# First attention: the products for one slot's maxima and for the next step of softmax put into shared four-bank tiles, five to a slot

## The chip, the cores and the metric

One core of a Trainium2 chip runs the whole program. The metric is the device time of one execution in microseconds (us), the median of several executions. Engines are named as in the profile: PE (TensorE, matrix products; PEld is its weight load), DVE (VectorE), ACT (ScalarE), POOL (GpSimd) and SP (the queue that issues most DMAs). SBUF is the on-chip memory that all of them read and write; PSUM is the memory that PE writes, in eight banks of 512 float32 columns on 128 partitions.

## What is computed

Two layers, each with an attention and a mixture of experts, on x of 8 batches x 512 tokens x 256 features, in float32. The change is in the first layer's attention, a causal softmax attention with 16 heads of 16 features:

```
xn = layernorm(x)
q, k, v = heads(xn @ Wq.T), heads(xn @ Wk.T), heads(xn @ Wv.T)   # 16 heads of 16
scores = where(causal, (q @ k.T) / 4, -inf)                      # 8 x 16 x 512 x 512
attn = softmax(scores, axis=-1)
x = x + (attn @ v) @ Wo.T + ffn(xn)                              # ffn: 8 experts, 2 a token, and a shared one
...                                                              # the second layer
```

The second layer is a gated linear attention, with experts of its own. It is the same in both kernels.

## The kernel before

**Slots.** The first attention is worked in 32 slots (`N = B * NG`): one slot is four heads of one batch. The four heads of a slot sit on four groups of 32 partitions of `q` and `k` (16 features, a row for the maximum, zeros), so that four products of 32 rows run on PE side by side. The loop (L1172) runs n from -1 to 32; in the part for n it takes the maxima of slot n + 1, the softmax weights of slot n, and its average.

**Two passes over the scores.** `maxima(n, j)` (L955) makes the scores of query tile j (128 queries) against its (j + 1) x 128 keys: four products, a head each (L961), then four products of an identity with a mask in bfloat16 that add a large negative number above the diagonal (L965). DVE takes the maximum over the keys (L966). `shift(n)` (L968) turns the four tiles' maxima on PE (L972) and subtracts them from q's spare rows on DVE (L978). `probs(n, i)` (L981) makes the transposed, shifted scores of key tile i against the 512 - 128 i queries from it on (L987), ACT takes exp from PSUM into SBUF (L991), and POOL clears what lies above the diagonal (L993). `average(n)` (L1004) multiplies the four exp tiles with v (L1011). `scaled(n)` (L1023) divides by the row sums on DVE, one slot later.

I write m3 to m0 for the maxima products of query tiles 3 to 0 (512, 384, 256, 128 keys), s0 to s3 for the weight products of key tiles 0 to 3 (512, 384, 256, 128 queries), and `red` and `exp` for the DVE and ACT instructions that read them.

**One PSUM tile.** All these scores go through the pool `l0sc`, which has one buffer (`bufs=1`) of four banks, a head to a bank. Every `maxima` and every `probs` takes it as a new tile, so PE may write the next one only when DVE or ACT has read the last one. In a slot the tile turns over eight times: m3, s0, m2, s1, m1, s2, m0, s3. The other four banks (`l0mm`) hold everything else, a bank each.

**What fills the gaps.** Between these steps the loop puts other work into the program: `fill(each)` takes steps from the list `between` (norms, router, values, output projections, the experts' second products gdn, L692, and the shared expert's, sdn, L1094, transposes xgTp, L600), seven times in a slot. After them come the projections qk (L931) of slot n + 2, the experts' first products gup (L659) or sup (L1071) and the average. `move(...)` lets POOL issue the indirect DMAs of the routing, after the last POOL mask. The order that each engine gets is made from this by a scheduler when the program is built: it moves single products of the filler in between, and it puts a wait before any instruction that writes a tile which another engine still reads. Each engine then runs its list strictly in order.

**ACT's tables.** exp and gelu (L677, L1078) use different tables of ACT. Where one follows the other, an ACT_TABLE_LOAD stands before it.

Of the kernel before, what the change touches and what calls it, by code (L numbers as in the profile page):

```python
# [8 lines left out]
F32 = mybir.dt.float32  # L9
# [3 lines left out]
ALU = mybir.AluOpType  # L13
AX = mybir.AxisListType
PSUM = bass.MemoryType.PSUM

B, S, D = 8, 512, 256
P = 128
NT = S // P
# [6 lines left out]
H0, HD0 = 16, 16  # L26
# [58 lines left out]
def tile_two_layers(  # L85
# [22 lines left out]
    nc = tc.nc  # L108
# [96 lines left out]
    last = {}  # L205
# [6 lines left out]
    @contextmanager  # L212
    def behind(*engines):
        with ExitStack() as stack:
            for e in engines:
                if e in last:
                    stack.enter_context(tc.issue_after(last[e].ins))
            yield
# [636 lines left out]
    with tc.tile_pool(name="l0w", bufs=1) as awp, tc.tile_pool(  # L855
        name="l0", bufs=2
    ) as ap, tc.tile_pool(name="l0e", bufs=2) as wp, tc.tile_pool(
        name="l0sc", bufs=1, space=PSUM
# [9 lines left out]
        mxs, vaugs = [], []  # L868
# [27 lines left out]
        N = B * NG  # L896
# [13 lines left out]
        def values(b, t):  # L910
            ps = ps_mm.tile([P, S], F32, tag="mm", name=f"v{b}_{t}")
            for k in range(KD):
                nc.tensor.matmul(
                    ps[:, :D],
                    xnT[b][:, k, t * P : (t + 1) * P],
                    wv[:, k, :],
                    start=(k == 0),
                    stop=(k == KD - 1),
                )
            nc.scalar.copy(  # L920
                vaugs[b % 2][:, t, : H0 * W].rearrange("p (h c) -> p h c", c=W)[:, :, :HD0],
                ps[:, :D].rearrange("p (h d) -> p h d", h=H0),
            )
# [28 lines left out]
                        raws[which][at + HD0 * h : at + HD0 * (h + 1), :],  # L952
                    )

        def maxima(n, j):  # L955
            w = (j + 1) * P
            q, k = qs[n % 2], ks[n % 2]
            ps = ps_sc.tile([P, 4, S], F32, tag="sc", name=f"m{n}_{j}")
            for h in range(4):
                r = slice(32 * h, 32 * h + 32)  # L960
                nc.tensor.matmul(  # L961
                    ps[:, h, :w], q[r, j * P : w], k[r, :w], start=True, stop=False
                )
            for h in range(4):
                nc.tensor.matmul(ps[:, h, j * P : w], ident_h, mask_lt, start=False, stop=True)  # L965
            last["dve"] = nc.vector.tensor_reduce(mxs[n % 2][:, j, :, HD0], ps[:, :, :w], AX.X, ALU.max)  # L966

        def shift(n):  # L968

# [8 lines left out]
            nc.vector.tensor_sub(q, qs[n % 2], ps)  # L978
            shifted[n] = q

        def probs(n, i):  # L981
            w = S - i * P
            q, k = shifted[n], ks[n % 2]
            ps = ps_sc.tile([P, 4, S], F32, tag="sc", name=f"s{n}_{i}")
            for h in range(4):
                r = slice(32 * h, 32 * h + 32)
                nc.tensor.matmul(  # L987
                    ps[:, h, :w], k[r, i * P : (i + 1) * P], q[r, i * P :], start=True, stop=True
                )
            e = ap.tile([P, 4, w], F32, tag=f"pt{i}", name=f"pt{n}_{i}", bufs=1)  # L990
            nc.scalar.activation(e, ps[:, :, :w], AF.Exp, scale=0.25)  # L991

            last["pool"] = nc.gpsimd.affine_select(  # L993
                out=e[:, :, :P],
                in_=e[:, :, :P],
                pattern=[[0, 4], [1, P]],
                base=0,
                channel_multiplier=-1,
                compare_op=ALU.is_ge,
                fill=0.0,  # L1000
            )
            pts[n, i] = e
# [20 lines left out]
        def scaled(n):  # L1023

            b, g = divmod(n, NG)
            if g == 0:
                oTs[b] = ap.tile([P, KD, S], F32, tag="oT", name=f"oT{b}", bufs=1)
            ou = ous.pop(n)
            den = ap.tile([P, S // 32], F32, tag="den", name=f"den{n}", bufs=1)
            nc.vector.reciprocal(den, ou[:, :, HD0])  # L1030
            nc.vector.tensor_mul(ou, ou, den.unsqueeze(2).to_broadcast([P, S // 32, 32]))
            rd = ap.tile([P, S], F32, tag="rd", name=f"rd{n}", bufs=1)
            nc.vector.transpose(rd, ou.rearrange("p n c -> p (n c)"))
            for h in range(4):
                at = (g % 2 * 4 + h) * HD0
                nc.sync.dma_start(
                    oTs[b][at : at + HD0, g // 2, :], rd[32 * h : 32 * h + HD0, :]
                )
# [80 lines left out]
        def groups_of(n):  # L1119
            if n < FIRST:  # L1120
                return [shared.popleft() for _ in range((2, 0, 0, 1, 2, 2, 2, 2, 1)[n + 1])]
            if n <= LAST:
                have = NG_MAX - len(experts)
                want = -(-NG_MAX * (n + 1 - FIRST) // (LAST + 1 - FIRST))
                return [experts.popleft() for _ in range(want - have)]
            return [shared.popleft() for _ in range(min(1, len(shared)))]
# [14 lines left out]
        def fill(n):  # L1141
            for _ in range(n):
                if between:
                    between.popleft()()

        def move(n):
            for _ in range(n):
                if moves:
                    with behind("pool"):
                        moves.popleft()()  # L1150
# [21 lines left out]
        for n in range(-1, N + 1):  # L1172
            b, g = divmod(n, NG)
            steps = []
            for _ in range(6 if n >= 0 else 2):
                if norms:
                    steps.append(norms.popleft())
            if n == 2:
                steps.append(routing)
            if n >= 1:  # L1180
                steps.append(lambda n=n: scaled(n - 1))
            if g == 1 and b + 1 < B:
                steps += [lambda b=b, t=t: values(b + 1, t) for t in range(NT)]
            for group in downs:
                steps += down_steps(group)
            groups = groups_of(n)
            if n == FIRST:
                loading()
            steps += [lambda i=i: routed.turn(i) for kind, i in groups if kind == "routed"]
            if n >= NG and g == 0:  # L1190
                steps += [lambda b=b, t=t: out(b - 1, t) for t in range(NT)]
            if n == -1:
                steps += [s for group in groups for s in up_steps(group)]
            if n == LAST + 2:
                move(len(moves))
                for i in range(2):
                    ask(i)
            if n > LAST + 1:
                steps += turn1_steps(ps_mm)
                for i in ((0,), (1, 2), (3, 4), (5, 6))[n - LAST - 2]:  # L1200
                    steps.append(lambda i=i: late(lambda: route0.add(i)))
                    if i + 2 < B:
                        steps.append(lambda i=i: ask(i + 2))
                    steps += [lambda s=s: late(s) for s in norm1_steps(i, ap)]
            if n == N:
                steps.append(lambda: route0.add(B - 1))
            between.extend(steps)
            each = -(-len(steps) // 7) if steps else 0
            pace = 2 if n < FIRST else 1

            if n == 10:
                load_second()
            if 0 <= n < N:
                shift(n)
            for s in range(NT):
                if n + 1 < N:
                    maxima(n + 1, NT - 1 - s)
                    move(pace)
                    fill(each)
                if 0 <= n < N:  # L1220
                    probs(n, s)
                    move(1)
                    if s < NT - 1:
                        fill(each)
            fill(len(between))
            if n + 2 < N:
                if n % 2 == 0:
                    for which in range(2):
                        project(n + 2, which)
                spread(n + 2)  # L1230
            elif n + 2 == N:
                with behind("spread"):
                    load_wcat()
            for group in groups:
                if n >= 0:
                    for step in up_steps(group):
                        step()
                kind, i = group
                if kind == "routed" and i in nxt:
                    routed.load(nxt[i])  # L1240
            if FIRST < n <= FIRST + CLEAR:
                clear(1, n - FIRST - 1)
            downs = groups
            if 0 <= n < N:
                average(n)
# [334 lines left out]
    with tc.tile_pool(name="m1w", bufs=4) as wp, tc.tile_pool(  # L1580
        name="m1", bufs=2
    ) as mp, tc.tile_pool(
        name="m1u", bufs=4, space=PSUM
    ) as ps_up, tc.tile_pool(name="m1d", bufs=2, space=PSUM) as ps_dn, tc.tile_pool(
        name="m1p", bufs=2, space=PSUM
# [105 lines left out]
```

## Time and profile before

| | |
|---|---|
| median of 8 executions | 1937.51 us (1934.67 to 1949.11) |
| the profiled execution | 1935.15 us, of which 1933.1 us are the span from the first to the last instruction |
| first attention, first to last slot | about 56 to 1019 us of the span |
| PE busy over the span | 1799.9 us (93%) |
| DVE, ACT, POOL busy | 831.2, 793.5, 401.1 us (43, 41, 21%) |
| granted PE clock, mean | 0.975 |

The profiled execution is 2.4 us below the median. In the profile's answers a group of instructions has its source line, its engine, what it writes and reads, a count, the busy time, the mean time of one in ns, and after the last bar the idle time of its engine just before it with what ended it. PE shows two records for a float32 product, one for a bfloat16 product or a transpose. A window gives the busy time of each engine in a stretch of the span, then the granted PE clock as a share of full speed.

### The profile page before, as it was taken

What the parts mean: (1) busy time and instruction counts of PE and PEld (TensorE: products, weight loads), DVE (VectorE), ACT (ScalarE), POOL (GpSimd) and SP (SyncE); (2) the same over time, 40 slices, a digit from 0 to 9 for tenths busy, and PEclk for the clock granted to TensorE, in tenths of its full rate; (3) what the DMA queues carried; (4) which work ended last, traced back from release to release, by engine and by line L of the source; (5) the groups of instructions that cost most, each with busy time, mean ns of one, the idle gap of its engine ahead of it and who ended that gap; (6) DMA issues with size and microseconds to landing.
All of it is one profiled execution on the core that took longest, in us unless ns stands there. A gap on an engine that the chain in (4) does not pass through costs nothing. (4 is left out here: it accounts for less than half of the span.)

```text
span 1933.1 us, 28227 instructions
## 1 busy us (share of the span) xinstructions
PE 1799.9 (93%) x10680; PEld 1232.0 (64%) x10680; DVE 831.2 (43%) x1886; ACT 793.5 (41%) x1452; POOL 401.1 (21%) x457
## 2 busy tenths in 40 slices
PE   5988999999999999999868899999999999999898
PEld 3434665666666665665434455598888998896455
DVE  5463334434444434444485877521111111115865
ACT  2333353454245445344443465342323233235455
POOL 2015441121122121121123274111111111111000
PEclk9998999999999999999879899999999999999999
DMA  8824221656534433342342141376676777662500
GB/s 244 196 56 134 84 90 46 202 161 185 178 121 134 148 121 134 105 158 73 115 145 68 45 142 59 108 256 231 229 274 216 258 261 250 218 259 82 163 12 23
DMA packets 163687, 289.17 MB, mean 150 GB/s; under 512 B 63952, under 2 KB 134624, under 8 KB 152928
## 3 DMA queue, kind: packets, MB, share of 16 engines
q1 hardware_dynamic: 148432, 248.77, 40.2%
q0 software_dynamic: 13088, 36.07, 5.2%
q10 hardware_dynamic: 2032, 2.54, 0.4%
q8 instruction: 84, 1.38, 0.3%
q14 instruction: 51, 0.42, 0.1%
HBM read 206.78 MB, written 67.94 MB: 142 GB/s over the span
## 5 line engine op out<-in xcount | busy, mean ns | idle before, releaser
L659 PE MATMUL gup<-xgT,ew 128*128 128x256 f32 (+1 forms) x2080 | 386.1, 338 | 4.7 <-DMA ew<-in_dram 2.4
L692 PE MATMUL gdn<-ew,hgT 128*128 128x256 f32 x1640 | 376.4, 383 | 0.0
L659 PEld LDWEIGHTS gup<-xgT,ew 128*128 128x128 f32 x2080 | 331.8, 192 | 47.5 <-issue 7.6
L692 PEld LDWEIGHTS gdn<-ew,hgT 128*128 128x128 f32 x1640 | 307.7, 191 | 50.8 <-issue 11.5
L966 DVE TENSOR_REDUCE mx<-m 128x4 f32<-128x2048 f32 (+3 forms) x128 | 190.3, 1486 | 270.6 <-PE m L965 270.4
L991 ACT ACTIVATE pt<-s 128x2048 f32<-128x2048 f32 (+3 forms) x128 | 158.3, 1237 | 196.4 <-PE s L987 195.8
L719 POOL DMA_INDIRECT zd<-yo,row x144 | 140.3, 974 | 466.8 <-DVE yo L710 403.7
L993 POOL TENSOR_SCALAR_AFFINE_SELECT pt<-pt 128x512 f32<-128x512 f32 x128 | 81.7, 638 | 664.6 <-ACT pt L991 664.6
L670 ACT ACTIVATE hgT<-gup,ew 128x256 f32<-128x256 f32 (+1 forms) x376 | 133.6, 422 | 208.9 <-issue 123.3
L710 DVE SCALAR_TENSOR_TENSOR yo<-ew,way,yo 128x256 f32<-128x256 f32 x72 | 31.7, 482 | 299.6 <-ACT yo L708 299.6
L961 PE MATMUL m<-k,q 32*128 32x512 f32 (+3 forms) x1024 | 124.5, 489 | 23.8 <-ACT pt L991 19.0
L437 POOL DMA_INDIRECT xd<-xr,pos x128 | 128.1, 1000 | 47.0 <-issue 41.9
L987 PE MATMUL s<-qsh,k 32*128 32x512 f32 (+3 forms) x1024 | 112.3, 496 | 25.2 <-DVE mx L966 24.7
L991 ACT ACT_TABLE_LOAD x52 | 66.7, 1283 | 118.7 <-PE s L987 117.8
L961 PEld LDWEIGHTS m<-k,q 32*128 32x128 f32 x1024 | 48.8, 186 | 82.1 <-ACT pt L991 53.8
L1011 PE MATMUL av<-pt,vaug 128*32 128x256 f32 (+3 forms) x1024 | 91.2, 459 | 5.9 <-POOL pt L993 5.7
L987 PEld LDWEIGHTS s<-qsh,k 32*128 32x128 f32 x1024 | 42.9, 191 | 82.7 <-DVE mx L966 63.9
L1020 DVE STREAM_TRANSPOSE ou<-av 128x512 f32<-128x512 f32 x32 | 22.9, 717 | 143.2 <-PE av L1011 143.1
L708 ACT ACTIVATE yo<-gdn,way 128x256 f32<-128x256 f32 x72 | 30.2, 472 | 125.9 <-PE gdn L692 125.7
L1433 PE MATMUL a<-qb,qkTs 128*128 128x512 f32 x128 | 67.3, 608 | 5.7 <-DVE qb L1426 3.7
L1419 PE MATMUL d<-u,cs 128*128 128x512 f32 x128 | 68.7, 619 | 3.9 <-ACT u L1402 3.9
L1402 ACT ACTIVATE u<-cs,lf 128x128 f32<-128x128 f32 x224 | 72.2, 394 | 0.0
(254 smaller groups left out, 2341.3 us busy)
## 6 DMA issues: line engine op xcount, KB each, us to landing
ew<-in_dram SPq DMA_DIRECT2D x47, 2180.0 KB
ew<-in_dram SPq DMA_DIRECT2D x36, 1024.0 KB
xd<-zero SPq DMA_DIRECT2D x12, 1572.0 KB
z<-zd SPq DMA_DIRECT2D x32, 512.0 KB
xnT<-in_dram SPq DMA_DIRECT2D x22, 512.0 KB
xg<-xd SPq DMA_DIRECT2D x36, 262.0 KB
xg<-xd SPq DMA_DIRECT2D x144, 64.0 KB
xn_d<-l_xn SPq DMA_DIRECT2D x16, 512.0 KB
```

What stands on the lines that cost most here:

```text
L437: i = nc.gpsimd.indirect_dma_start(out=self.xd, out_offset=bass.IndirectOffsetOnAxis(ap=self.pos[k][:, at : at + 1], axis=0), in_=held[b][ ...
L659: nc.tensor.matmul(ps[:, j, at : at + m], wu[u][:, k, f * P : (f + 1) * P], x, start=(k == 0), stop=(k == KD - 1),)
L670: nc.scalar.activation(ht[:, f, at : at + m], ps[:, j, at : at + m], AF.Gelu, bias=w[u][2][:, f : f + 1],)
L692: nc.tensor.matmul(ps[:, t, :], ht[:, f, t * P : (t + 1) * P], wd[:, f, :], start=(f == 0), stop=(f == nf - 1),)
L719: d = nc.gpsimd.indirect_dma_start(out=self.r.zd, out_offset=bass.IndirectOffsetOnAxis(ap=row[:, s : s + 1], axis=0), in_=y[:, s, :], in_o ...
L961: nc.tensor.matmul(ps[:, h, :w], q[r, j * P : w], k[r, :w], start=True, stop=False)
L966: last["dve"] = nc.vector.tensor_reduce(mxs[n % 2][:, j, :, HD0], ps[:, :, :w], AX.X, ALU.max)
L987: nc.tensor.matmul(ps[:, h, :w], k[r, i * P : (i + 1) * P], q[r, i * P :], start=True, stop=True)
L991: nc.scalar.activation(e, ps[:, :, :w], AF.Exp, scale=0.25)
L993: last["pool"] = nc.gpsimd.affine_select(out=e[:, :, :P], in_=e[:, :, :P], pattern=[[0, 4], [1, P]], base=0, channel_multiplier=-1, compar ...
L1011: nc.tensor.matmul(ps[32 * h : 32 * h + 32, i * P :], vaugs[b % 2][:, i, c : c + 32], e[:, h, :], start=(i == 0), stop=(i == NT - 1),)
L1402: nc.scalar.activation(u[:, h, :], inc, AF.Copy, scale=lf[:, c, h : h + 1])
```

## The change

A tile of `l0sc` is now taken five times in a slot, and `maxima` and `probs` get it handed in. The first holds m3 alone and the second s0 alone (both use all 512 columns of each bank); the other three hold s3 with m2, s2 with m1, and s1 with m0: the weights' products in the first columns of each bank and the maxima's in the last ones, 512 columns together. The key tiles come in the order 0, 3, 2, 1, the query tiles in the order 3, 2, 1, 0 as before. `fill` is called five times in a slot, each with a fifth of the steps, and `move` five times. The number and the sizes of the products, reductions and exps stay.

```
-        def maxima(n, j):
+        def maxima(n, j, ps):
...
-            ps = ps_sc.tile([P, 4, S], F32, tag="sc", name=f"m{n}_{j}")
+            ps = ps[:, :, S - w :]
...
-            last["dve"] = nc.vector.tensor_reduce(mxs[n % 2][:, j, :, HD0], ps[:, :, :w], AX.X, ALU.max)
+            last["dve"] = nc.vector.tensor_reduce(mxs[n % 2][:, j, :, HD0], ps, AX.X, ALU.max)
...
-        def probs(n, i):
+        def probs(n, i, ps):
             w = S - i * P
             q, k = shifted[n], ks[n % 2]
-            ps = ps_sc.tile([P, 4, S], F32, tag="sc", name=f"s{n}_{i}")
...
-            each = -(-len(steps) // 7) if steps else 0
+            each = -(-len(steps) // 5) if steps else 0
...
-            for s in range(NT):
-                if n + 1 < N:
-                    maxima(n + 1, NT - 1 - s)
-                    move(pace)
-                    fill(each)
-                if 0 <= n < N:
-                    probs(n, s)
-                    move(1)
-                    if s < NT - 1:
-                        fill(each)
+            for s in range(NT + 1):
+
+                j = (NT - 1, None, 2, 1, 0)[s] if n + 1 < N else None
+                i = (None, 0, 3, 2, 1)[s] if 0 <= n < N else None
+                if j is None and i is None:
+                    continue
+                ps = ps_sc.tile([P, 4, S], F32, tag="sc", name=f"sc{n}_{s}")
+                if i is not None:
+                    probs(n, i, ps)
+                if j is not None:
+                    maxima(n + 1, j, ps)
+                move(pace + 1 if s else 1)
+                fill(each)
```

More of the change, by code (lines that the diff above doesn't have):

```diff
@@ L953, in spread @@
                     )
-        def maxima(n, j):
+        def maxima(n, j, ps):
             w = (j + 1) * P
             q, k = qs[n % 2], ks[n % 2]
-            ps = ps_sc.tile([P, 4, S], F32, tag="sc", name=f"m{n}_{j}")
+            ps = ps[:, :, S - w :]
             for h in range(4):
                 r = slice(32 * h, 32 * h + 32)
-                nc.tensor.matmul(
-                    ps[:, h, :w], q[r, j * P : w], k[r, :w], start=True, stop=False
-                )
+                nc.tensor.matmul(ps[:, h, :], q[r, j * P : w], k[r, :w], start=True, stop=False)
             for h in range(4):
                 nc.tensor.matmul(ps[:, h, j * P : w], ident_h, mask_lt, start=False, stop=True)
-            last["dve"] = nc.vector.tensor_reduce(mxs[n % 2][:, j, :, HD0], ps[:, :, :w], AX.X, ALU.max)
+            last["dve"] = nc.vector.tensor_reduce(mxs[n % 2][:, j, :, HD0], ps, AX.X, ALU.max)
         def shift(n):
```

## The prediction, made before the changed kernel ran

> **What bounds the kernel now.** I read the page's busy shares first, then PE by windows over the slots, then PE's groups by form for its waits, then the timeline of one slot.
>
> ```profile
> PE 1799.9 (93%) x10680; PEld 1232.0 (64%) x10680; DVE 831.2 (43%) x1886; ACT 793.5 (41%) x1452; POOL 401.1 (21%) x457
> ```
>
> ```profile
> 304.00:512.00 208.00, 203.50 (x1420) 132.26 (x1420) 88.54 (x166) 89.33 (x101) 39.83 (x51) 0.99 0.57 162
> 512.00:544.00 32.00, 29.78 (x182) 19.20 (x180) 11.51 (x23) 14.59 (x15) 6.03 (x8) 0.89 0.33 112
> 750.00:777.00 27.00, 24.13 (x196) 15.09 (x188) 11.78 (x22) 15.00 (x15) 4.36 (x6) 1.00 0.26 82
> 897.00:1019.00 122.00, 98.07 (x595) 53.15 (x593) 76.62 (x177) 51.13 (x57) 25.45 (x27) 0.86 0.36 114
> ```
>
> PE is the bound in the slots: 203.5 of 208 us in the middle ones. DVE and ACT are under half busy, so what matters of them is only when PE waits for them. The last slots (897 to 1019) have little filler, and PE idles there for 24 us. In the groups by form, the idle time before each product of the shared tile shows who was waited for:
>
> ```profile
> L987 PE MATMUL s<-qsh,k 32*128 32x512 f32 x256 | 38.7, 645 | 12.3 <-DVE mx L966 12.1
> L961 PE MATMUL m<-k,q 32*128 32x384 f32 x248 | 32.0, 533 | 2.2 <-ACT pt L991 2.2
> L987 PE MATMUL s<-qsh,k 32*128 32x384 f32 x256 | 31.9, 545 | 4.1 <-DVE mx L966 3.9
> L987 PE MATMUL s<-qsh,k 32*128 32x256 f32 x256 | 24.4, 453 | 4.7 <-DVE mx L966 4.6
> L961 PE MATMUL m<-k,q 32*128 32x256 f32 x248 | 22.7, 435 | 4.4 <-ACT pt L991 4.4
> L987 PE MATMUL s<-qsh,k 32*128 32x128 f32 x256 | 17.3, 342 | 4.1 <-DVE mx L966 4.1
> L961 PE MATMUL m<-k,q 32*128 32x128 f32 x248 | 16.3, 334 | 12.4 <-ACT pt L991 12.4
> L1011 PE MATMUL av<-pt,vaug 128*32 128x128 f32 x248 | 13.3, 288 | 3.1 <-POOL pt L993 2.9
> ```
>
> So PE waits 44.2 us for the tile (the first seven rows) and about 6 us for POOL before the averages. That 44 us is all that a better tile could give; the products themselves stay.
>
> **What one turnover costs.** From the timeline of the slot at 605 to 631 us:
>
> ```profile
> 621.70 0.40 PE L965 MATMUL m<-mask_lt,ident_h 128*128 128x128 bf16 x4
> ...
> 621.93 0.66 PE L659 MATMUL gup<-xgT,ew 128*128 128x128 f32 x4
> 622.13 1.23 DVE L966 TENSOR_REDUCE mx<-m 128x4 f32<-128x1024 f32 x1 [3.82 <-PE m L965]
> ...
> 623.64 0.71 PE L987 MATMUL s<-qsh,k 32*128 32x256 f32 x8
> ...
> 624.47 1.28 ACT L991 ACT_TABLE_LOAD   x1 [1.62 <-PE s L987]
> ...
> 624.61 2.75 PE L659 MATMUL gup<-xgT,ew 128*128 128x256 f32 x12
> 625.76 1.02 ACT L991 ACTIVATE pt<-s 128x1024 f32<-128x1024 f32 x1
> ...
> 627.30 0.50 PE L961 MATMUL m<-k,q 32*128 32x128 f32 x8
> ```
>
> After m1's masks PE goes on at 621.93; the reduction ends at 623.36 and PE may write 0.05 later: PE needs 1.48 us of other work to lose nothing, and has 1.71. After s2 it goes on at 624.29 and is released at 626.83, so it needs 2.54 us, of which 1.28 are the table load that a gelu in between forces; it has 3.01. In the same way from the other forms (reductions 2.25, 1.76, 1.23, 0.69 us; exps 1.88, 1.45, 1.02, 0.60; lags as here) the need is 2.51, 2.02, 1.49, 0.94 us after m3, m2, m1, m0 and 2.11, 1.70, 1.27, 0.90 after s0, s1, s2, s3, each 1.28 more with a load. Filler: twelve records of 256 columns from 624.61 to 627.30, 0.22 each; so 0.43 a product of 256, 0.86 of 512, 0.22 of 128, and 0.11 a transpose.
>
> **What the change does to the turnovers.** Five tiles should mean five turnovers. The order and the waits of the built program say otherwise: in each shared tile the maxima's first product waits for ACT, and the count it waits for is that of the exp of the same tile. PE may not write into banks that ACT still reads, though the columns differ. So the chain in a slot is m3, s0, s3, exp, m2, red, s2, exp, m1, red, s1, exp, m0, red: still eight turnovers with the same eight readers. The number of PE products is equal too, and the last 2349 of PE's instructions stand in the same order. What changes is which reader comes when, and what filler PE has behind it.
>
> The Trainium skill ("PSUM — Partial Sum Buffer", on bank collisions) says that accesses by two engines must be kept apart by bank and 32-partition group, not by address. That speaks against the change; no row of before has two engines in one bank. By that rule the saving is nothing, which is also what the built order gives.
>
> I went through both built orders, turnover by turnover, and took need minus filler where positive. Two examples. **m2 to s2**, slots 11, 13, 15: before, m2 was followed by two gdn products and eight transposes (1.74 against 2.02, loss 0.3); now s2 follows after the eight transposes alone (0.88, loss 1.1). **Slot 7** (and 23 alike): before, s2 to m0 had three average products against 2.55, loss 2.07 (1.71 in the trace); now nothing stands between m1 and s1 (loss 1.48 in slot 7, 0.63 in 23) nor between s1 and m0, where the 384-wide exp with its load needs 2.98. Over slots 0 to 31:
>
> | turnover behind | m3 | m2 | m1 | m0 | s0 | s1 | s2 | s3 |
> |---|---|---|---|---|---|---|---|---|
> | before, worked out | 0.6 | 3.0 | 4.7 | 5.6 | 4.5 | 7.8 | 13.5 | 0.0 |
> | before, in the trace | 12.3 | 4.1 | 4.7 | 4.1 | 2.2 | 4.4 | 12.4 | - |
> | changed, worked out | 0.8 | 8.3 | 9.1 | 0.0 | 4.7 | 20.1 | 7.3 | 1.8 |
>
> Without m3 (where DVE's transposes and divisions of the slot before stand ahead of the reduction, in both orders) this is 39.1 before and 51.3 changed: 12.2 us more. The trace has 31.9 for the 39.1, a factor of 0.82, so I take **+10 us**. Most of it is in the slots with little filler (1, 7, 23, 27, 29, 30: 9 us).
>
> **Other terms.** POOL: the average waited 5.9 us in all for the mask of s3's exp, the last before it; now the last exp is followed by m0 and the first average products, so I take half, **-3 us** (bounds -6 and 0). Table loads: the built ACT order has four fewer (5 us of ACT), but those that stand right behind products are in the table above. `move` gives POOL 9 or 13 places a slot for 8 or 12: nothing, POOL is 21% busy, and without that cover a later indirect DMA is about 1 us. DVE: the m1 reduction now stands nearer to the twelve small operations and two copies (about 3 us) behind the transposes; in the slots with two expert groups these can delay it by 0.2 to 0.9 us, but before has the same by the same count (22 now, 26 before), so 0, between -4 and +5.
>
> **The clock.** Between 512 and 544 us the granted clock is 0.89: one wait of 2.06 us for a DMA cost another 32 x 0.11 = 3.5 us. Between 750 and 777, with 1.71 us as the longest gap, it is 1.00. The gaps of about 3 us in slots 7 and 23 lie beyond the first row, which is the nearer one. I take +3 us for both together (slot 7 is followed by a half-speed stretch already), bounds 0 and +17 (five slots at 3.5: 3, 7, 23, 29, 30).
>
> The Trainium skill ("TensorE: Matmul & The Clock Gate", Part 1) has the clock fall after an idle window of about 3.4 us; by that alone the 2.06 us would have cost nothing, which the row contradicts. By the page the clock term would be 0 and the sum about 7.
>
> **Sum:** 10 - 3 + 3 = +10 us. On the profiled execution that is 1935.15 + 10 = about 1945; it was 2.4 below the median, so on the median 1937.5 + 10 = **1947.5 us**.
>
> **Rivals.**
> - *Not slower: the waits are moved, not added.* In the slots with little filler the chain through the tile sets the length, not PE; its eight links are unchanged, so the 9 us there need not be paid, and what remains (3.2 x 0.82 = 2.6) is met by POOL's -3 to -6: 1934 to 1938. For it: the last slots idle for 24 us. Against it: even there PE was 80% busy, and the loss in slots 7 and 23 is PE's. It decides if these slots grow by under 0.5 us each. A gain of over 0.3% would need the DVE term at its -4 besides: 1930.
> - *The clock falls in all five slots.* 10 - 3 + 17 = +24: 1961.
> - *The change does what it says*, if m need not wait for the exp of its tile: m2, m1 and m0 would follow at once and three turnovers go. Of 32 us between s0 and m0 perhaps 15 to 20 would go: 1918 to 1922. The waits of the built program exclude it but for a misreading.
>
> **How the numbers follow.** Forecast (+6 to +16) 0.55, clock rival 0.17, moved waits 0.25 (of which 0.06 faster), as it says 0.03. A change of 0.3% (5.8 us) is about what a measurement of this kernel can tell from none. Slower by more: 0.55 + 0.17 = 0.72; faster: 0.06 + 0.03 = 0.09; within: 0.19. Range 1936 to 1962: from the moved waits to the clock rival.
>
> **What would show it.** Right: the maxima's products of 384, 256 and 128 keys show waits for ACT, the last of them near 20 us; s2 and s1 (256, 384 queries) wait near 9 us each for DVE; slots 7 and 23 are 2 us longer, with a lower clock. Wrong: a maxima product that starts while the exp of its tile runs, or the waits for the tile together at or under 44 us.

## The result and the profile after

The changed kernel takes 1954.48 us (median of 16 executions, 1947.32 to 1956.66) beside 1936.59 us for the kernel before on the same chip: a ratio of 1.0086, 95% interval 1.0075 to 1.0098. On the 1937.5 us of the prediction that is +17, where +10 was forecast. The profiled execution took 1961.1 us with a span of 1959.4. It lies 6.6 us above the median, and above the slowest of the 16 (1956.66), so the two profiles differ by 26 us and not by 17. From the first to the last slot's transposes (mT), the kernel before takes 932.3 us and the changed one 954.9. Most of the time is lost in these slots of the first attention, and the rest of the span differs by 3.7 us. Windows of the two kernels over these slots (length, then PE, PEld, DVE, ACT and POOL busy, then PE's clock, the DMA share and GB/s), before first:

```profile
56.50:988.80 932.30, 875.53 (x5953) 541.12 (x5953) 403.99 (x753) 393.44 (x439) 219.90 (x272) 0.97 0.42 127
```

```profile
56.40:1011.30 954.90, 869.07 (x5961) 544.26 (x5961) 408.03 (x753) 388.18 (x436) 220.64 (x273) 0.96 0.41 124
```

PE is idle for 932.3 - 875.5 = 56.8 us before and for 954.9 - 869.1 = 85.8 us after: 29.0 more. It is also busy for 6.5 us less. The groups by form of the changed kernel's PE in the slots say what it waited for:

```profile
L964 PE MATMUL sc<-k,q 32*128 32x512 f32 x248 | 45.6, 683 | 9.4 <-DMA k<-raw 7.9 <-issue 1.4
L987 PE MATMUL sc<-qsh,k 32*128 32x512 f32 x256 | 37.5, 640 | 11.5 <-DVE mx L967 11.5
L987 PE MATMUL sc<-qsh,k 32*128 32x384 f32 x256 | 33.7, 570 | 12.1 <-DVE mx L967 11.9
L1011 PE MATMUL av<-pt,vaug 128*32 128x384 f32 x256 | 31.4, 567 | 1.3 <-POOL pt L993 1.3
L964 PE MATMUL sc<-k,q 32*128 32x384 f32 x248 | 29.5, 533 | 1.0 <-ACT pt L991 1.0
L987 PE MATMUL sc<-qsh,k 32*128 32x256 f32 x256 | 25.3, 444 | 17.6 <-DVE mx L967 17.6
L964 PE MATMUL sc<-k,q 32*128 32x256 f32 x248 | 23.2, 444 | 6.1 <-ACT pt L991 6.1
L987 PE MATMUL sc<-qsh,k 32*128 32x128 f32 x256 | 17.5, 321 | 2.2 <-ACT pt L991 2.2
L964 PE MATMUL sc<-k,q 32*128 32x128 f32 x248 | 16.7, 341 | 23.8 <-ACT pt L991 23.8
```

The seven waits for the tile come to 74.3 us where there were 44.2. Each maxima product of a shared tile (384, 256, 128 keys) waits for ACT, which is the exp of the same tile: the tile still turns over eight times. m0 (128 keys) now waits for s1's exp, s2 and s1 (256 and 384 queries) for the reductions of m2 and m1. The averages' wait for POOL is nearly gone. The first row is new: m3 waited 7.9 us for the copies of k, where it waited 2.9.

**Slot 4** alone grows from 34.3 to 42.5 us, as its windows say, before first:

```profile
185.50:219.80 34.30, 34.10 (x216) 21.79 (x212) 12.44 (x16) 9.80 (x11) 19.77 (x24) 0.97 0.36 116
189.30:231.80 42.50, 37.05 (x209) 24.11 (x205) 12.44 (x16) 9.21 (x10) 17.33 (x20) 0.87 0.28 89
```

The timeline of PE and of SP's queue in the changed kernel (start, duration; in brackets the idle time before and what ended it):

```profile
195.70 3.91 PE L964 MATMUL sc<-k,q 32*128 32x512 f32 x8 [5.45 <-DMA k<-raw]
199.54 0.60 PE L966 MATMUL sc<-mask_lt,ident_h 128*128 128x128 bf16 x4
```

```profile
181.46 0.59 SPq L431 DMA_DIRECT2D xr<-xn_d  x1
193.69 2.42 SPq L950 DMA_DIRECT2D k<-raw  x4
```

Between the two SP lines, the answer on line 524 (reads of the experts' numbers into SP's registers) for 182 to 193.65 us has:

```profile
L524 SPq TENSOR_LOAD <-eid x18: 262/272/662, 182.1 to 193.1; - x18
L524 SPq FUSED_REGOPS  x18: 147/147/154, 182.7 to 193.4; - x18
```

Eighteen reads in 11.5 us, 0.64 from one to the next, stand in SP's queue ahead of k's copy. The last products that read this k tile (s1 of slot 3, at 181.90) ended at 182.8, so the reads held the copy up by as much as 10.8 us. In the kernel before the same queue shows this, with no read between the lines:

```profile
181.06 0.59 SPq L431 DMA_DIRECT2D xr<-xn_d  x1
185.65 2.42 SPq L950 DMA_DIRECT2D k<-raw  x4
```

Its reads had gone through ahead of the first of these lines (19 from 169.9 to 180.2 us). The scheduler puts these reads, which only wait for the routing, wherever its plan has room; the change altered the plan. From 193.4, 3.2 us into PE's gap, the granted clock is 0.50 for 10.2 us, of which the last 7.9 are work:

```profile
193.40:203.60 10.20, 7.90 (x21) 5.32 (x22) 2.29 (x1) 0.00 (x0) 0.00 (x0) 0.50 0.28 79
```

The Trainium skill ("TensorE: Matmul & The Clock Gate", Part 1) has the clock halved after an idle window of about 3.4 us. This gap agrees with it: PE was busy for 0.25 us of the 3.4 before the fall.

**Slot 6** shows the same kind of thing on DVE. Its timeline in the changed kernel:

```profile
277.65 0.21 POOL L432 COPY xr<-of 128x24 f32<-128x24 f32 x1
277.89 0.28 DVE L288 TENSOR_SCALAR of<-cs 128x32 f32<-128x32 f32 x2 [3.88 <-POOL xr L432]
278.07 1.75 DVE L967 TENSOR_REDUCE mx<-sc 128x4 f32<-128x1536 f32 x1
...
279.88 0.71 PE L987 MATMUL sc<-qsh,k 32*128 32x256 f32 x8 [2.77 <-DVE mx L967]
```

A small operation of the second layer's routing (L288) may not overwrite `of` before POOL's copy has read it, and the reduction of m2 stands behind it. In the kernel before, the operation came after m0's reduction (at 276.08, 1.75 us of waiting), with no reduction behind it in the way.

**Slot 2** has the longest wait of s2, 5.8 us, again for m2's reduction. There a long row of small operations of the routing (130 to 142.6 us) stands in DVE's queue ahead of it. In the kernel before it stood ahead of the same reduction, and s1 waited 3.0 us. Before first:

```profile
143.93 1.66 PE L987 MATMUL s<-qsh,k 32*128 32x384 f32 x8 [3.03 <-DVE mx L966]
144.40 1.23 PE L987 MATMUL sc<-qsh,k 32*128 32x256 f32 x8 [5.82 <-DVE mx L967]
```

### The profile page after: what moved, and what is told of

The parts are those of the page before. It is cut to its first block, busy times and chain, and to the rows that moved or that the text cites. A ratio compares the mean times of both kernels' runs of the same rounds, so it can differ in the third digit from the quotient of the medians.

```text
span 1959.4 us, 28400 instructions
## 1 busy us (share of the span) xinstructions
PE 1798.4 (92%) x10680; PEld 1238.2 (63%) x10680; DVE 832.3 (42%) x1886; ACT 787.8 (40%) x1448; POOL 403.7 (21%) x457
## 5 line engine op out<-in xcount | busy, mean ns | idle before, releaser
L967 DVE TENSOR_REDUCE mx<-sc 128x4 f32<-128x2048 f32 (+1 forms) x124 | 184.1, 1485 | 243.3 <-PE sc L966 241.5
L991 ACT ACTIVATE pt<-sc 128x2048 f32<-128x2048 f32 (+3 forms) x128 | 158.3, 1237 | 213.5 <-PE sc L987 212.9
L987 PE MATMUL sc<-qsh,k 32*128 32x512 f32 (+3 forms) x1024 | 113.9, 493 | 43.4 <-DVE mx L967 41.0
L964 PE MATMUL sc<-k,q 32*128 32x512 f32 (+1 forms) x992 | 115.0, 500 | 40.3 <-ACT pt L991 30.9
L987 PEld LDWEIGHTS sc<-qsh,k 32*128 32x128 f32 x1024 | 43.3, 187 | 97.5 <-DVE mx L967 72.6
L964 PEld LDWEIGHTS sc<-k,q 32*128 32x128 f32 x992 | 45.9, 191 | 92.1 <-ACT pt L991 72.1
L1011 PE MATMUL av<-pt,vaug 128*32 128x512 f32 (+3 forms) x1024 | 88.6, 481 | 1.3 <-POOL pt L993 1.3
L1020 DVE STREAM_TRANSPOSE ou<-av 128x512 f32<-128x512 f32 x32 | 22.9, 717 | 109.7 <-PE av L1011 109.7
```

Of the source, the lines that this page charges most:

```text
L964: nc.tensor.matmul(ps[:, h, :], q[r, j * P : w], k[r, :w], start=True, stop=False)
L987: nc.tensor.matmul(ps[:, h, :w], k[r, i * P : (i + 1) * P], q[r, i * P :], start=True, stop=True)
L1011: nc.tensor.matmul(ps[32 * h : 32 * h + 32, i * P :], vaugs[b % 2][:, i, c : c + 32], e[:, h, :], start=(i == 0), stop=(i == NT - 1),)
```

## The experiments

**The theories.** *A*: sharing does nothing, and the time comes from filler, because five places for it in place of seven leave too little behind some turnovers. *C*: it comes from the order of the readers (long ones late in the slot, and m0 behind the wide exp of s1), whatever the number of places. *B* and *D*: it comes from the in-order queues of SP (the reads of L524) and DVE (L288). *S* is B and D together. Further rivals: sharing itself costs, or saves.

Each set of four ran on one chip beside the kernel before; ratios are to that. On all three chips the kernel before took about 2000 us (medians 1999.22, 2000.24 and 2002.90), so only ratios and differences within a set are used. A *hold* below records an instruction as not to be issued ahead of the last q or k copy (SP) or the last reduction (DVE) recorded before it.

### Set 1

**The changed order with a tile for each block** (`e1_own8`):

```
-                ps = ps_sc.tile([P, 4, S], F32, tag="sc", name=f"sc{n}_{s}")
...
-                    probs(n, i, ps)
+                    probs(n, i, ps_sc.tile([P, 4, S], F32, tag="sc", name=f"s{n}_{i}"))
...
-                    maxima(n + 1, j, ps)
+                    maxima(n + 1, j, ps_sc.tile([P, 4, S], F32, tag="sc", name=f"m{n}_{j}"))
```

> The changed kernel's order and five places for filler, but every maxima and weights block has a score tile of its own again (eight tiles a slot); the instructions stand on PE, ACT, DVE and SP in exactly the changed kernel's order. Theory A (the time comes from the order of the readers and the filler behind them, sharing a tile's columns does nothing, good or bad): the same as the changed kernel within 0.3%, ratio 1.006 to 1.011, waits for the tile together 71 to 77 us as against 74.3. Rival (sharing itself costs, since two readers hold one tile's banks): faster than the changed kernel by over 6 us, ratio under 1.005. Rival (sharing saves a turnover somewhere): slower, ratio over 1.012.

Measured: 1.0086 (1.0055 to 1.0118), 6 runs in two groups (2007 to 2009 and 2020 to 2022 us). The waits for the tile are 79.9 us, and 79.7 for the changed kernel on such a chip (set 3); they lie above the expected 71 to 77 by what the rows of s0 and s1 gained on this chip (14.2 and 14.5 us for 11.5 and 12.1). Sharing neither saves nor costs a turnover: what the change moved is the order and the places alone. By time alone, sharing is excluded only to within the interval. The PE waits of this kernel in the slots (us in total, times, longest):

```profile
PE s L987 <- DVE mx L967: 43.7, 43, 5.8
PE m L964 <- ACT pt L991: 31.6, 26, 4.0
```

**The changed kernel with the hold on SP's reads** (`e1_after_sp`):

```
-            e = nc.sync.value_load(r.eid[0:1, u : u + 1], min_val=0, max_val=7)
+            with behind("spread"):
+                e = nc.sync.value_load(r.eid[0:1, u : u + 1], min_val=0, max_val=7)
```

> The changed kernel, in which the reads of the expert numbers (L524) stay behind the q and k copies in SP's order instead of being hoisted in front of them; PE, ACT and DVE have the changed kernel's order. Rival B (SP's in-order queue): the wait of 5.45 us for k in slot 4 and the 10.2 us of half clock behind it go, slot 4 is 34 to 36 us long instead of 42.5, and the whole is 6 to 9 us shorter than the changed kernel: ratio 1.004 to 1.006. Theory A alone (all of the added time is short filler behind turnovers): no difference, ratio 1.007 to 1.010. Both say that the waits for the tile stay at 71 to 77 us.

Measured: 1.0031 (1.0010 to 1.0052); median 2004.86 against 2014.23 us for the kernel above, 9 less, though the comparison is with the eight-tile form and its two groups. Slot 4 is 33.8 us long (39.7 in `e1_own8`), and m3's waits in all the slots are 0.1 us (3.4, of them 1.9 for k). B holds as a part. The waits for the tile are as large as ever (82.0 us).

**Before with the same hold** (`e1_before_sp`), the same edit on the kernel before:

> The kernel before with the same hold on the reads of the expert numbers. Rival B in its strict form (SP's delay is what the change brought, and the kernel before had none in its slots): no gain, ratio 0.998 to 1.002. If the queue cost the kernel before something too (its k wait of 2.06 us in slot 15 with a half clock behind it, 3.0 us of k waits in all): 3 to 6 us, ratio 0.997 to 0.9985.

Measured: 0.9992 (0.9972 to 1.0012). The hold alone gives the kernel before nothing that can be told.

**The hold, and seven places** (`e1_fill7_sp`), on top of the changed kernel with the hold:

```
-            each = -(-len(steps) // 5) if steps else 0
+            each = -(-len(steps) // 7) if steps else 0
...
                     probs(n, i, ps)
+                    move(1)
+                    fill(each)
...
-                move(pace + 1 if s else 1)
-                fill(each)
+                    move(pace)
+                    if s < NT:
+                        fill(each)
```

> The changed kernel with the hold on SP's reads and, besides, a place for filler between the weights and the maxima of a shared tile (seven places with a seventh each, as before the change; the order m3, s0, s3, m2, s2, m1, s1, m0 of the changed kernel stays). Theory A (too little filler behind m1, s1 and m2 because there are only five places): the waits for the tile fall from 74 to 45 to 55 us and the time is 15 to 25 us under the changed kernel, ratio 0.996 to 1.002. Rival C (it is the order of the weights, with the 384-wide exp and its table load last, that costs, and not the number of places): the waits stay over 65 us, and the time is that of the run with the hold alone, ratio 1.003 to 1.006.

Measured: 1.0043 (1.0024 to 1.0063), not better than without the places, and the waits for the tile are 81.1 us. In the changed order A falls: m0 waits as long as in the changed kernel. Its groups by form:

```profile
L988 PE MATMUL sc<-qsh,k 32*128 32x384 f32 x256 | 33.5, 581 | 12.9 <-DVE mx L968 12.7
L988 PE MATMUL sc<-qsh,k 32*128 32x256 f32 x256 | 23.4, 435 | 13.4 <-DVE mx L968 13.4
L965 PE MATMUL sc<-k,q 32*128 32x128 f32 x248 | 17.1, 349 | 23.8 <-ACT pt L992 23.8
```

### Set 2

**Before's order, five places** (`e2_old5_sp`), with the hold:

```
-            each = -(-len(steps) // 7) if steps else 0
+            each = -(-len(steps) // 5) if steps else 0
...
-                    move(pace)
-                    fill(each)
+                    if s == 0:
+                        move(1)
+                        fill(each)
                 if 0 <= n < N:
                     probs(n, s)
-                    move(1)
-                    if s < NT - 1:
-                        fill(each)
+                move(pace + 1)
+                fill(each)
```

> Eight tiles in the order of before (m3, s0, m2, s1, m1, s2, m0, s3) with the hold on SP's reads, but only five places for filler with a fifth of the steps each (behind m3, s0, s1, s2 and s3), as the changed kernel has them. It is the place count alone. Theory A (too few places): the waits for the tile rise from the 54 us of before with the hold to over 65 us, ratio 1.002 to 1.005. Rival C (the order of the readers costs, the places hardly do): waits within 6 us of 54, ratio 0.997 to 1.001.

Measured: 1.0092 (1.0059 to 1.0125), 6 runs, yet the profiled execution has 54.3 us of waits for the tile, as before with the hold (53.5). The two speak against each other: by the waits the number of places costs nothing, by the time 0.9%. The profiled execution was the fastest of the six (2006.58 us, median 2016.72); what the others lost, no profile shows. Left open: it doesn't bear on the waits, but in before's order a cost of the five places, as large as that of the whole change, is not excluded.

**Only the order of the weights** (`e2_w0321_sp`), seven places, eight tiles, the hold:

```
-                    probs(n, s)
+                    probs(n, (0, 3, 2, 1)[s])
```

> Eight tiles, seven places and the hold on SP's reads as in before with the hold; only the weights come in the changed kernel's order, s0, s3, s2, s1: the chain is m3, s0, m2, s3, m1, s2, m0, s1. It is the order of the weights without what sharing does to it (s1 ahead of m0). Rival C in its strict form (the 384-wide exp with its table load late in the slot costs wherever it stands): ratio 1.002 to 1.005. Rival C by neighbours (what costs is that m0 comes directly behind s1 and s1 behind m1): m0 is behind s2 again and waits 11 to 15 us in all as before, waits for the tile 48 to 58 us, and only POOL's wait ahead of the averages grows, since the mask of s1's exp is then the last: 6 us before, 8 to 16 now; ratio 0.999 to 1.003.

Measured: 1.0060 (1.0037 to 1.0082). C holds in its strict form. m0 waits as little as in before (10.3 us for ACT), but s1, now last, waits 17.9 us, and s0's row has 26.6 (21.4 in before with the hold, on another chip). The averages' wait for POOL does not grow (0.1), against what I expected. Its groups by form:

```profile
L988 PE MATMUL s<-qsh,k 32*128 32x384 f32 x256 | 35.0, 594 | 17.9 <-DVE mx L967 12.4 <-ACT pt L992 5.5
L962 PE MATMUL m<-k,q 32*128 32x128 f32 x256 | 16.7, 332 | 11.6 <-ACT pt L992 10.3 <-DVE mx L967 1.3
```

**Filler shared out evenly over before's seven places** (`e2_even7_sp`), with the hold:

```
-                    fill(each)
+                    fill((2 * s + 1) * len(steps) // 7 - 2 * s * len(steps) // 7)
...
-                        fill(each)
+                        fill((2 * s + 2) * len(steps) // 7 - (2 * s + 1) * len(steps) // 7)
```

> Before with the hold on SP's reads, and the steps of a slot shared out evenly over its seven places (0 or 1 more each) instead of a seventh rounded up at each, which leaves the last places of the slots with 8 to 11 steps or with 2 to 5 empty or thin. If filler at the right place is what the turnovers lack: waits for the tile 54 to under 45 us, ratio 0.994 to 0.998. If the scheduler moves the filler to where it is needed anyhow: within 5 us of before with the hold, ratio 0.998 to 1.001.

Measured: 1.0009 (0.9986 to 1.0032), waits for the tile 51.3 us. No gain: the scheduler moves the filler, and the places in the program hardly bind it.

**Both holds on the changed kernel** (`e2_after_sp_of`), SP's and on DVE:

```
+                with behind("dve"):
                     nc.vector.tensor_scalar_add(
                         self.of[:, :, 1, k], rowno[:, :TT], 1.0 + k * PLANE
                     )
```

> The changed kernel with the hold on SP's reads and with one small DVE operation of the routing (L288) held behind the last reduction recorded before it, so that it no longer stands ahead of a reduction in slot 6, where it waited 3.88 us for a transfer and PE lost 2.77 us behind it. PE, ACT and SP have the order of the run with the hold alone. Rival D (DVE's in-order queue): the wait of s2 in slot 6 goes to 0 and the time is 2 to 5 us below that run, ratio 1.001 to 1.002. Theory A: no difference, ratio 1.003.

Measured: 1.0010 (0.9987 to 1.0033). s2's row falls from 16.1 to 14.8 us with the second hold, since slot 6 no longer has a wait there (1.3 us in the run with one hold). But slot 6 is no shorter for it, 35.2 us beside 34.3 (on another chip), and the 5.8 us of slot 2 stay, which this hold doesn't touch. In time, D (1.001 to 1.002) fits, but the interval also takes in the 1.0031 of the first hold alone: not told apart.

### Set 3

**The changed kernel again** (`e3_after`), no edit:

> The changed kernel itself again, unaltered, as the anchor for the three others of this set. Expected from its first runs: ratio 1.0075 to 1.0098. If the chip adds to it as much as the eight-tile twin showed: 1.0055 to 1.0118.

Measured: 1.0044 (1.0023 to 1.0066), median 2011.50 us. The change costs less on this chip than on the first one, and the intervals do not meet. Its slots are no shorter in the profile than on the first chip (958.6 us from the first to the last mT, 954.9 there); what the kernel before has on this chip that it hasn't on the first was not profiled.

**Both holds again** (`e3_after_sp_of`), the edits above:

> The changed kernel with both holds (SP's reads of expert numbers, and the one DVE operation of the routing). Theory S (most of the added time is what the in-order queues of SP and DVE let ahead of a k copy and of a reduction): 8 to 15 us under the changed kernel of the same set, ratio 1.001 to 1.004. Theory A and C (the turnovers of the score tile carry most of it): under 6 us, ratio 1.005 to 1.009.

Measured: 0.9998 (0.9978 to 1.0018), median 2003.19 us: 8.3 less than the changed kernel, at the lower end of S's 8 to 15.

**Both holds on before** (`e3_before_sp_of`), the same edits:

> The kernel before with both holds. It lost nothing to these two queues in its slots, so theory S expects no change, ratio 0.998 to 1.001; what then remains between this run and the changed kernel with the same holds, 3 to 8 us, is the price of the turnovers. If the holds help by themselves, whatever the tiles: ratio under 0.997.

Measured: 0.9969 (0.9943 to 0.9995), median 1997.28 us. The two holds together help the kernel before as well, by 5.6 us, which S did not expect. What remains between the kernels with equal queues is 2003.19 - 1997.28 = 5.9 us; the intervals of the two ratios overlap, and the two profiled executions (1999.36 and 2000.35 us) differ by 1.0 the other way.

**Both holds, the shared tiles in the opposite order** (`e3_rev_sp_of`), on the changed kernel with both holds:

```
-                j = (NT - 1, None, 2, 1, 0)[s] if n + 1 < N else None
-                i = (None, 0, 3, 2, 1)[s] if 0 <= n < N else None
+                j = (NT - 1, None, 0, 1, 2)[s] if n + 1 < N else None
+                i = (None, 0, 1, 2, 3)[s] if 0 <= n < N else None
```

> The changed kernel with both holds and its three shared tiles in the opposite order: s1 with m0, s2 with m1, s3 with m2 (chain m3, s0, s1, m0, s2, m1, s3, m2). Five tiles and five places as before. Theory C (what the change pays is the wide exp with its table load at the end of a slot, where the filler has run out: m0 behind s1 waited 24 to 26 us in all): m0's wait falls under 12 us, that of m2 behind s3's exp stays under 12, waits for the tile from 81 us to under 65, ratio 0.995 to 1.000. Rival: the reduction of m2 (1.76 us) now stands last, and the next slot's transposes and s0 wait for it: waits of mT for DVE appear and the ratio is 1.003 or more.

Measured: 0.9887 (0.9845 to 0.9929), 6 runs (1968.08 to 1989.89), median 1985.97 us: 17 under the kernel before, 17 under the changed kernel with the same holds and 11 under the kernel before with the same holds. It is the fastest version here. The windows over the slots of the changed kernel with holds, before with holds, and this one (it splits a slot's four transposes, so its window runs from the last two of the first slot to the last two of the last):

```profile
56.30:998.30 942.00, 860.51 (x5961) 539.04 (x5961) 407.97 (x753) 388.01 (x436) 220.64 (x273) 0.96 0.42 126
```

```profile
56.30:993.50 937.20, 871.38 (x5952) 540.66 (x5952) 404.27 (x753) 392.99 (x439) 220.02 (x272) 0.97 0.42 127
```

```profile
58.70:989.50 930.80, 871.90 (x5976) 540.99 (x5976) 404.45 (x743) 383.66 (x429) 219.32 (x272) 0.98 0.42 127
```

PE idles for 81.5, 65.8 and 58.9 us, and these slots are 11.2 us shorter than in the changed order and 6.4 shorter than in before's. The last average ends at 1025.9, 1025.7 and 1013.7 us of the span. PE's waits there, in the same three kernels (us in total, times, longest):

```profile
PE sc L989 <- DVE mx L969: 40.5, 41, 5.8
PE sc L966 <- ACT pt L993: 32.3, 25, 3.0
```

```profile
PE s L989 <- DVE mx L968: 31.9, 34, 3.9
PE m L963 <- ACT pt L993: 18.9, 14, 2.9
PE av L1013 <- POOL pt L995: 4.1, 7, 1.8
PE m L963 <- DMA k<-raw: 2.8, 2, 2.1
PE wo L1045 <- DMA oT<-rd: 2.6, 3, 1.5
```

```profile
PE sc L989 <- DVE mx L969: 27.0, 36, 2.6
PE sc L966 <- ACT pt L993: 12.4, 15, 3.2
PE sc L989 <- ACT pt L993: 4.5, 4, 2.2
PE mT L975 <- DVE mx L969: 2.6, 2, 2.2
```

By rows of the groups, m0 waits 9.3 us (25.8 with the holds in the changed order), s2 1.5 (14.8), s1 4.5 (13.7), and mT 2.7 (0.9). In this order s2 follows m0's short reduction and not m2's long one, and m2's stands last, where only the transposes and s0 wait for it: s0's row grows to 22.9 us (15.2). With s0 and mT, the waits come to 49.5 us, where the changed order with the holds has 79.7 and before with the holds 53.6. Five tiles are not shown to be the cause: the same order with eight tiles, or without the holds, was not run.

**All runs together.** Waits for the tile without s0's row, which follows m3 in every kernel (s0's row lies between 11.5 and 26.6 us and varies within an order too; with it the orders come to 44 to 54, 69, 74 to 82 and 47 us):

| order | kernels | us |
|---|---|---|
| before (m3 s0 m2 s1 m1 s2 m0 s3) | before; hold; five places; even places; both holds | 31.9; 32.1; 34.7; 33.7; 33.1 |
| s0 s3 s2 s1 in between | `e2_w0321_sp` | 42.1 |
| changed (m3 s0 s3 m2 s2 m1 s1 m0) | after; again; eight tiles; hold; both holds (sets 2 and 3); seven places | 62.8; 65.9; 65.7; 63.1; 64.0, 63.6; 57.4 |
| opposite | `e3_rev_sp_of` | 23.9 |

The order sets them; tiles and holds move them by 3 us at most, places by 6.

## Why the prediction was right or wrong

**Sign and range: right.** +17 us of the forecast's +10, inside 1936 to 1962. That the sum came this close is in part luck: as the next paragraphs show, the waits grew by three times the term, much of that was not time, and a loss in SP's queue was not in the sum.

**Eight turnovers: right**, and the signs it named came: maxima products wait for ACT, m0 for 23.8 us ("near 20"), s1 for 12.1 ("near 9"). s2 waited 17.6, twice what was said. `e1_own8` shows that sharing does nothing. So "the change does what it says" is out. A form in which the weights and the maxima of a tile lie in different banks was not tried.

**The turnover term: mis-sized, by two errors that partly cancel.** It worked out 12.2 us more waiting and took 0.82 of it. Measured, without s0's row, are 62.8 - 31.9 = 30.9. By turnover, worked out and measured: behind m1 9.1 and 12.1, behind m2 8.3 and 17.6, behind s1 20.1 and 23.8, behind s2 7.3 and 6.1, behind s3 1.8 and 1.0, behind s0 4.7 and 2.2. Only m2 is far off, and 8.6 of its 17.6 us come from slots 2 and 6, where DVE's queue held routing operations ahead of the reduction (in slot 2 the kernel before paid 3.0 for them, in s1's row).

The other error is that waiting was taken for time. With equal queues the two kinds of wait for the tile grow from 50.8 to 72.8 us in the lists above, the total idle time only by 15.7, the slots by 4.8, the time by 5.9 on the medians, and the last average ends at the same time. The other waits shrink (POOL, k, oT: the rows in the second list), and PE is busy for 10.9 us less. Of these, 6.7 are in the products of m3 (from 47.8 to 41.1 us): a group of eight that takes 1.14 us at its shortest takes up to 2.5 in the kernel before with the holds, at full clock, it seems because the later heads wait for their copies of k, and the profile counts that as busy.

"The waits are moved, not added", a rival with 0.25, fails by its own sign: of the slots that it names (1, 7, 23, 27, 29, 30) all but the last grew by over 0.5 us, 11.7 together, and 7.0 together with equal queues (there slot 7 shrank by 0.5). But it is right in part: with equal queues slots 4, 8, 15, 24 and 28 are each 2 to 3 us shorter.

**SP: the step that was missing.** The sum has no term for SP's queue, though the change moves where everything is planned. Slot 4 costs 8.2 us through it, 5.45 of waiting and then half clock. The hold on the reads takes 9 us from the changed order with eight tiles to the changed kernel in set 1, and nothing that can be told from before.

**DVE: taken as 0, between -4 and +5.** Slots 2 and 6 alone put 8.6 us of waiting into s2's row, 5.6 more than the kernel before had from the same operations; what that is worth in time was not resolved.

**POOL: right.** -3 forecast, 5.7 to 1.3 measured.

**The clock: right in kind, wrong in place.** Slots 7 and 23 grow by 4.2 and 2.0 us, with the clock at 0.94 in each where it was 0.99 and 1.00. Most of that is waiting, though: PE idles for 3.2 and 1.4 us more there and is busy for 0.9 and 0.6 more, and in slot 8 the clock rose (0.95 to 1.00). The largest loss is slot 4's, which no step foresaw; the clock also fell in slots 2 (0.84 to 0.75), 3 (0.97 to 0.89) and 29 (0.84 to 0.77), and rose in slot 15 (0.89 to 1.00).

**How the parts add up.** On the chip of set 3, order 5.9 us and queues 8.3 less the 5.6 that before gains too. Each ratio has an interval of 4 us or more either way, differences a wider one, and the first chip, with +17, was not met again. That both mechanisms are there is shown: the order by the waits and by two runs (only the weights' order changed, 1.0060; the opposite order, 0.9887), SP's queue by the hold. Their shares of the 17 us are not, and what made `e2_old5_sp` slow is not known.

## What to carry to other kernels

Where a tile is handed from reader to reader, the waits hung here on which reader stood where the filler ran out. It paid to put the short ones there and a long one where only late work follows. Ask of a reordering what the scheduler does with every in-order queue, register reads and foreign small operations included, since a queue that the change doesn't touch can cost several microseconds (8.2 in slot 4). And a wait that is added is not time that is added: look for the waits that it replaces, those counted as busy too.

## What the runs showed of the hardware

Reads of an expert's number into a register followed each other in SP's queue at 0.57 us (19 in the kernel before) to 0.64 us (18 in the changed one), and eighteen of them kept a copy waiting for up to 10.8 us. One gap of PE of 5.45 us brought 10.2 us at half clock, which began 3.2 us into the gap.

The same kernel took 3% longer on three other chips, and, as far as a profile shows it, mostly not in the part that was changed: after the last slot's transposes the span has 944.4 us in the kernel before on the first chip, and 1004.8 in the kernel before with both holds on the chip of set 3. There PE idles for 50 of the 150 us from 1080 to 1230 (9 on the first chip), and its clock falls (the window 1130 to 1180, that chip and then the first one):

```profile
1130.00:1180.00 50.00, 27.79 (x105) 16.29 (x106) 13.71 (x34) 13.43 (x34) 25.01 (x29) 0.64 0.36 123
```

```profile
1130.00:1180.00 50.00, 48.14 (x249) 27.77 (x249) 36.85 (x77) 28.43 (x74) 39.54 (x41) 1.00 0.41 138
```

What held them there, the profile does not name (it puts 37.7 us of DVE's and 32.5 of ACT's waits down to "remote").
